# Layer 0 of a four-layer convolution chain: a step's outputs gathered in one block behind the next step's first scores, hidden units on four banks, two key turns together

## The chip, the cores and the metric

The program runs on one core of one Trainium2 chip. The metric is the device time of one execution in microseconds (us); lower is better. The kernel before was timed three times: 6459.06 us is the median, 6456.72 and 6465.38 us are the ends. One more execution was profiled and took 6479.63 us.

## What is computed

Four layers run one after the other on an image batch x of 4 x 16 x 512 x 512 floats. The change touches layer 0 alone:

```python
x = x + depthwise_conv3x3(x)                  # "position"
xt = tokens(x)
q, k, v = qkv(affine1(xt)), in 8 x 8 windows, 2 heads of 8 channels
x = xt + proj(softmax(q k^T / sqrt(8)) v)     # attention within each window
x = x + fc2(gelu(fc1(affine2(x))))            # 16 -> 64 -> 16 channels
```

Layer 1 quantizes its input (by the largest absolute value of layer 0's output), convolves, normalizes by batch statistics and clips; layers 2 and 3 are convolutions with additions. They take the second half of the time and are not changed.

## The kernel before, in words

**Tiling.** `window_attention` (L154) computes layer 0. The image is cut into 64 steps (`STEPS`, L177). A step holds 256 windows: 128 partitions are 4 strips `vv` of 32, and along the free dimension lie 4 images `u` of 512 tokens each (8 windows of 64). PSUM has eight banks: `bank(0)` to `bank(3)` are two pairs, `bank(4)` to `bank(7)` are singles (L182 to L186).

**The parts of a step n**, in the order in which they are written out by hand (loop at L469; the schedule of TensorE, VectorE, ScalarE and SyncE is manual, L451, so each engine works through its instructions in the order of the text):

- `values(k, n)` (L342), for k = 0 to 7: four 128 x 128 transposes of the keys' tile `y2` on TensorE into bank 4 or 6, then a copy on VectorE into `yt`.
- `scores(k, n)` (L355): sixteen matmuls with tiles of 32 rows by 128 columns into banks 0 to 3, then two exponentials of 1024 columns on ScalarE.
- `attend(k, n)` (L374): sixteen matmuls of 128 rows by 32 columns for the weighted sums and four more for the denominators; `divide` (L389): a logarithm and an exponential on ScalarE, one product on VectorE.
- The loop for k = 1 to 7 (L479) writes scores of k, attend of k - 1, values of k, divide of k - 1. So TensorE has scores, attend, values in turn. At odd k `turn_keys` (L316) sends eight DMAs on SyncE's queue, which bring the next step's keys into `y2`.
- `queries` (L326) for the next step, twice, and `project` (L399), both with tiles of 32 x 32.
- The second half, here called the unit stretch (L506 to L515): 52 places. A place is either a `hidden` unit (L412: four matmuls of 32 x 32 tiles into one of the banks 4, 5, 6, then a Gelu on ScalarE) or four matmuls of the depthwise convolution of step n + 2 (L291, banks 0 to 3). Places go round the four row groups of the array. Hidden units stand at places 4, 7, 10 and so on, every third; there are 16 of them and 36 depthwise places.
- `output` (L425): four matmuls of 128 rows by 32 columns into bank 7, then an addition on VectorE into `xo`; in odd steps `store` (L437) follows: one maximum over 1024 columns on VectorE (L439) and sixteen DMAs on SyncE's queue to the DRAM tile `x1` (L96). Outputs stand at four points of a step: after hidden units 5 and 9, behind the unit stretch, and (the last four hidden units) behind the next step's first scores (L476).
- `position(n + 2)` (L302) empties banks 0 to 3: two of them on VectorE, two on ScalarE. ScalarE loads the table for exponentials at L471, after that, and the Gelu table with the first Gelu of a step.

After the last step a bound on the scores is computed (L523 to L535, with two reductions over partitions on GpSimd); a flag from it decides whether another attention routine runs. Then the convolution layers start.

Of the kernel before, what the change touches and what calls it, by code (L numbers as in the profile page):

```python
# [1 line left out]

# [22 lines left out]
P = 128  # L25
# [5 lines left out]
NH, HD = 2, 8  # L31
WS = 8
# [51 lines left out]
        nc.sync.dma_start(part[:, at : at + m, :], src[:, a : a + m, :])  # L84


def _store_block(nc, x1, src, b, r0, cols):

    n = WS // 2
    s, m = divmod(r0 // 2, M)  # L90
    parts = [(1, m, s, 0, n), (0, m + 1, s, 0, n)]
    if m + n == M and s < S - 1:
        parts[1:] = [(0, m + 1, s, 0, n - 1), (0, 0, s + 1, n - 1, 1)]
    for r, mm, ss, at, k in parts:
        part = 32 * b + C * r
        nc.sync.dma_start(  # L96
            x1[mm : mm + k, part : part + C, ss, cols].rearrange("m c x -> c m x"),
            src.rearrange("c (m r) x -> c m r x", r=2)[:, at : at + k, 1 - r],
        )
# [54 lines left out]
def window_attention(ctx: ExitStack, tc, xw, x1, hots, m, v, peak):  # L154
# [78 lines left out]
    with tc.tile_pool(name="w0s", bufs=1) as scratch:  # L233
# [10 lines left out]
        size = wts.tile([P, NH + 1], F32, name="size")  # L244
# [27 lines left out]
    px = ctx.enter_context(tc.tile_pool(name="w0x", bufs=2))  # L272
# [69 lines left out]
    def values(k, n):  # L342

        vv, jl = k // 2, 4 * (k % 2)
        b = bank(4 + 2 * (k % 2))
        for jj in range(4):
            nc.tensor.transpose(  # L347
                b[:, P * jj : P * jj + P],
                y2[:, vv, jl + jj].rearrange("p w t -> p (w t)"), m("ident"),
            )  # L350
        t = px.tile([P, 4, P], F32, tag="yt", name=f"yt{n}_{k}", bufs=3)
        nc.vector.tensor_copy(t.rearrange("p j c -> p (j c)"), b)  # L352
        return t

    def scores(k, n):  # L355

        vv, jl = k // 2, 4 * (k % 2)
        for jj in range(4):
            for u in range(U):
                nc.tensor.matmul(  # L360
                    bank(u)[:, P * jj : P * jj + P],
                    y2[quad(u), vv, jl + jj].rearrange("p w t -> p (w t)"),
                    g[quad(u), vv, jl + jj].rearrange("p h t -> p (h t)"),
                    start=True, stop=True,
                )
        e = px.tile([P, U, 4, P], F32, tag="e", name=f"e{n}_{k}", bufs=3)
        for i in range(2):
            nc.scalar.activation(  # L368
                e[:, 2 * i : 2 * i + 2].rearrange("p u j t -> p u (j t)"),
                pairs[i], AF.Exp,  # L370
            )
        return e

    def attend(e, yt, k):  # L374

        b, d = bank(4 + 2 * (k % 2)), bank(5 + 2 * (k % 2))
        for jj in range(4):
            for u in range(U):
                nc.tensor.matmul(  # L379
                    b[quad(u), P * jj : P * jj + P], yt[:, jj, quad(u)], e[:, u, jj, :],  # L380
                    start=True, stop=True,
                )
        for u in range(U):
            nc.tensor.matmul(  # L384
                d[quad(u)], own, e[:, u].rearrange("p j t -> p (j t)"),
                start=True, stop=True,
            )
# [21 lines left out]
                y[:, u], bank(4 + u), pb, y[:, u], ALU.add, ALU.add  # L409
            )  # L410

    def hidden(y, q, n):  # L412

        u, vv = q // 4, 3 * q % 4
        b = bank(4 + q % 3)
        for k in range(4):
            nc.tensor.matmul(  # L417
                b[quad(k)], fc1[quad(vv), quad(k)], y[quad(vv), u, :],
                start=True, stop=True,
            )  # L420
        hd = px.tile([P, N], F32, tag="hid", name=f"hid{n}_{u}_{vv}", bufs=8)
        nc.scalar.activation(hd, b, AF.Gelu, bias=f1b)  # L422
        return vv, hd

    def output(y, xo, hids, u, n):  # L425
        b = bank(7)
        for vv, hd in hids:
            nc.tensor.matmul(b[quad(vv)], m("fc2"), hd, start=True, stop=True)  # L428
        at = BW * (n % 2)
        nc.vector.tensor_tensor(  # L430
            xo[:, u, :, at : at + BW].rearrange("p a (j x) -> p a j x", x=WS),
            by_window(b), by_window(y[:, u]), ALU.add,
        )
        if n % 2:
            store(xo, n // 2, u)

    def store(xo, k, u):  # L437
        i, cb = divmod(k, NQ)
        nc.vector.tensor_reduce(  # L439
            peak[:, U * k + u : U * k + u + 1], xo[:, u], AX.XY, ALU.max,  # L440
            apply_absolute_value=True,
        )
        for vv in range(V):
            for w in range(2):
                r = SR * (2 * vv + w) + WS * i
                _store_block(
                    nc, x1, xo[32 * vv + C * w : 32 * vv + C * w + C, u], u, r,
                    slice(XW * cb, XW * cb + XW),
                )

    ctx.enter_context(  # L451
        tc.manual_schedule(
# [13 lines left out]
    for h in range(NH):  # L466
        queries(ys[0], h)
    last, xo = None, None
    for n in range(STEPS + 1):  # L469
        if n < STEPS:  # L470
            nc.scalar.preload_act_table_set("natural_log_exp_and_others")  # L471
# [5 lines left out]
        if n == STEPS:  # L477
            break
# [44 lines left out]
    top = wts.tile([P, 1], F32, name="top")  # L523
    nc.vector.tensor_reduce(top, most, AX.X, ALU.max)
    ytop = wts.tile([P, 1], F32, name="ytop")
    nc.gpsimd.partition_all_reduce(ytop, top, P, bass_isa.ReduceOp.max)
    sized = wts.tile([P, NH + 1], F32, name="sized")
    nc.gpsimd.partition_all_reduce(sized, size, P, bass_isa.ReduceOp.add)
    bound = wts.tile([P, 1], F32, name="bound")
    nc.vector.tensor_tensor(bound, sized[:, 0:1], sized[:, 1:2], ALU.max)  # L530
    nc.vector.tensor_scalar(bound, bound, ytop, sized[:, 2:3], ALU.mult, ALU.add)
    nc.vector.tensor_scalar(bound, bound, ytop, 1.0 / 8.0, ALU.mult, ALU.mult)
    flag = wts.tile([P, 1], mybir.dt.int32, name="flag")
    nc.vector.tensor_scalar(flag, bound, 40.0, None, ALU.is_le)
    return nc.values_load(flag[0:1, 0:1], min_val=0, max_val=1)  # L535


# [816 lines left out]
```

## Time and profile before

| What | us |
|---|---|
| median of three runs | 6459.06 |
| the profiled execution | 6479.63 |
| its span | 6477.8 |
| first transposes of layer 0's step 1 and of step 63 start at | 122.6 and 3479.5 |
| one step, from transposes to transposes | 54.12 |
| layer 0's last output matmuls start at | 3539.8 |
| last stores of layer 0 issued until | 3564.3 |
| first VectorE instruction of the convolution layers at | 3568.8 |

TensorE's matmul row is busy for 96% of the span, VectorE for 50%, ScalarE for 63%. A busy matmul row doesn't mean that TensorE does as much as it can: matmuls overlap, and their ends are modelled. The row of weight loads (PEld) tells more, since every matmul has its own load right ahead of it; where loads stop, TensorE can't take the next instruction. A 32-bit matmul appears as two loads and two matmul records. In the timeline each line gives the start, the duration, the engine, the source line, the operation with the shape of its tile (rows by columns of the array), what is written and read, the number of instructions, and in brackets how long the engine was idle before and what ended that.

Between steps 2 and 61 every step has the same pattern, and nearly every one takes 54.10 to 54.15 us. Its parts, read from the starts of the weight loads of one such step:

| Part of a step | us |
|---|---|
| values 0, scores 0, output of the step before, scores 1 | 0.59, 1.38, 1.25, 2.00 |
| attend 0 with denominators | 1.87 |
| six times values, scores, attend | 6 x 3.56 |
| values 7, queries, attend 7, queries and project | 0.59, 1.07, 1.90, 3.90 |
| unit stretch in three pieces | 6.25, 3.40, 5.57 |
| the outputs behind these pieces | 1.00 each |

### The profile page before, as it was taken

What the parts mean: (1) busy time and instruction counts of PE and PEld (TensorE: products, weight loads), DVE (VectorE), ACT (ScalarE), POOL (GpSimd) and SP (SyncE); (2) the same over time, 40 slices, a digit from 0 to 9 for tenths busy, and PEclk for the clock granted to TensorE, in tenths of its full rate; (3) what the DMA queues carried; (4) which work ended last, traced back from release to release, by engine and by line L of the source; (5) the groups of instructions that cost most, each with busy time, mean ns of one, the idle gap of its engine ahead of it and who ended that gap; (6) DMA issues with size and microseconds to landing.
All of it is one profiled execution on the core that took longest, in us unless ns stands there. A gap on an engine that the chain in (4) does not pass through costs nothing. (4 is left out here: it accounts for less than half of the span.)

```text
span 6477.8 us, 317011 instructions
## 1 busy us (share of the span) xinstructions
PE 6215.1 (96%) x146976; PEld 3422.4 (53%) x146976; DVE 3208.4 (50%) x4713; ACT 4062.8 (63%) x5602; POOL 130.9 (2%) x89
## 2 busy tenths in 40 slices
PE   8999999999999999999998569999999999999999
PEld 4555555555555555555553335555555555555554
DVE  3444444444444444444443564555555555555555
ACT  4777777777777777777775443444444444444444
POOL 0000000000000000000000520000000000000000
PEclk9999999999999999999998679999999999999999
DMA  3333333333333333333232752222222222222221
GB/s 80 62 72 61 72 61 72 61 72 61 72 61 72 60 73 61 72 60 73 59 58 36 295 181 75 83 82 82 83 84 86 81 81 81 81 86 82 83 74 51
DMA packets 568966, 515.30 MB, mean 80 GB/s; under 512 B 349008, under 2 KB 480208, under 8 KB 547152
## 3 DMA queue, kind: packets, MB, share of 16 engines
q1 hardware_dynamic: 567344, 494.52, 29.4%
q8 instruction: 1154, 18.91, 1.2%
q14 instruction: 180, 1.47, 0.1%
q10 hardware_dynamic: 288, 0.39, 0.0%
HBM read 225.87 MB, written 134.48 MB: 56 GB/s over the span
## 5 line engine op out<-in xcount | busy, mean ns | idle before, releaser
L1139 PE MATMUL tb<-y,mat 32*32 32x512 f32 x16384 | 1494.9, 596 | 6.5 <-issue 6.0
L1145 ACT ACTIVATE hid<-tb,vec 128x512 f32<-128x512 f32 x1280 | 829.5, 688 | 1068.3 <-PE tb L1139 1066.1
L368 ACT ACTIVATE e<-pair 128x1024 f32<-128x1024 f32 x1024 | 992.3, 1021 | 225.7 <-PE pair L360 225.0
L296 PE MATMUL pair<-x,taps 32*32 32x512 f32 x18432 | 968.2, 606 | 1.8 <-ACT y L307 1.2
L1147 DVE TENSOR_SCALAR hid<-tb,vec 128x512 f32<-128x512 f32 x768 | 574.4, 748 | 745.1 <-PE tb L1139 737.3
L417 PE MATMUL bank<-y,fc_e 32*32 32x512 f32 x8192 | 878.5, 607 | 3.7 <-ACT hid L422 3.1
L422 ACT ACTIVATE hid<-bank,f1b 128x512 f32<-128x512 f32 x1024 | 679.4, 686 | 298.4 <-PE bank L417 284.7
L352 DVE COPY yt<-bank 128x512 f32<-128x512 f32 x512 | 353.7, 691 | 905.6 <-PE bank L347 905.6
L360 PE MATMUL pair<-g,y 32*128 32x128 f32 x16384 | 652.1, 285 | 39.7 <-ACT e L368 38.7
L909 PE MATMUL tb<-z,cw 32*32 32x512 f32 x12864 | 634.6, 599 | 5.3 <-issue 4.1
L360 PEld LDWEIGHTS pair<-g,y 32*128 32x128 f32 x16384 | 541.4, 186 | 186.0 <-ACT e L368 108.8
L296 PEld LDWEIGHTS pair<-x,taps 32*32 32x32 f32 x18432 | 459.2, 103 | 288.5 <-issue 183.6
L1139 PEld LDWEIGHTS tb<-y,mat 32*32 32x32 f32 x16384 | 464.1, 103 | 270.7 <-issue 152.5
L909 PE MATMUL tb<-h,cw 32*32 32x512 f32 x12672 | 571.1, 597 | 3.5 <-ACT z L1078 1.5
L909 PE MATMUL tb<-q,cq 32*32 32x512 bf16 x12672 | 424.2, 458 | 151.3 <-issue 98.9
L909 PE MATMUL tb<-x,cw 32*32 32x512 f32 x12480 | 562.5, 597 | 2.0 <-ACT z L1078 1.4
L379 PE MATMUL bank<-e,yt 128*32 128x128 f32 x16384 | 555.3, 276 | 0.9 <-ACT r L394 0.9
L384 PE MATMUL bank<-e,hot 128*32 128x512 f32 x4096 | 534.4, 592 | 0.0
L379 PEld LDWEIGHTS bank<-e,yt 128*32 128x32 f32 x16384 | 417.7, 109 | 108.1 <-DVE yt L352 52.8
L1155 PE MATMUL tb<-hid,mat 128*32 128x512 f32 x4096 | 452.7, 594 | 0.0
L430 DVE TENSOR_TENSOR xo<-bank,y 128x512 f32<-128x512 f32 x256 | 177.0, 691 | 546.6 <-PE bank L428 544.7
L347 PEld LDWEIGHTS bank<-mat,y 128*128 128x128 f32 x2048 | 215.1, 141 | 430.1 <-issue 376.5
(158 smaller groups left out, 6731.7 us busy)
## 6 DMA issues: line engine op xcount, KB each, us to landing
x<-in_xw_dram SPq DMA_DIRECT2D x32, 2600.0 KB, 10.2
y<-y SPq DMA_DIRECT2D x2048, 32.0 KB, 2.1
tx<-x SPq DMA_DIRECT2D x64, 1024.0 KB, 5.7
xi<-x SPq DMA_DIRECT2D x1024, 64.0 KB, 2.1
out_dram<-xi SPq DMA_DIRECT2D x64, 1024.0 KB, 5.9
x<-xo SPq DMA_DIRECT2D x2000, 32.0 KB, 1.7
y<-x SPq DMA_DIRECT2D x24, 1024.0 KB, 5.5
xi<-x SPq DMA_DIRECT2D x24, 1024.0 KB, 5.2
```

The costliest lines, as they stand in the source:

```text
L296: nc.tensor.matmul(bank(u)[quad(vv)], taps[quad(u), tap, :], xts[n // 2][quad(u), vv, dy : dy + WS, at : at + BW], start=tap == 0, stop=ta ...
L360: nc.tensor.matmul(bank(u)[:, P * jj : P * jj + P], y2[quad(u), vv, jl + jj].rearrange("p w t -> p (w t)"), g[quad(u), vv, jl + jj].rearra ...
L368: nc.scalar.activation(e[:, 2 * i : 2 * i + 2].rearrange("p u j t -> p u (j t)"), pairs[i], AF.Exp,)
L379: nc.tensor.matmul(b[quad(u), P * jj : P * jj + P], yt[:, jj, quad(u)], e[:, u, jj, :], start=True, stop=True,)
L384: nc.tensor.matmul(d[quad(u)], own, e[:, u].rearrange("p j t -> p (j t)"), start=True, stop=True,)
L417: nc.tensor.matmul(b[quad(k)], fc1[quad(vv), quad(k)], y[quad(vv), u, :], start=True, stop=True,)
L422: nc.scalar.activation(hd, b, AF.Gelu, bias=f1b)
L909: nc.tensor.matmul(p[i][_quad(j)], weights[_quad(i), side, dx, :], src[side][_quad(i), j, dx : dx + W], start=side == 0 and dx == 0, stop= ...
L1139: nc.tensor.matmul(p[_quad(c)], w1[_quad(b), 1 - par, 32 * c : 32 * c + 32], inner(ys(mm + par))[_quad(b), s, :], start=True, stop=True,)
L1145: nc.scalar.activation(hd, p, AF.Relu, bias=v("l3_b1"))
L1147: nc.vector.tensor_scalar(hd, p, v("l3_b1"), 0.0, ALU.add, ALU.max)
L1155: nc.tensor.matmul(p[_quad(b), :], w2[:, par], hd, start=par == 0, stop=par == 1)
```

## The change

- A step's sixteen output matmul groups (four per image, all four images) stand in one block, into banks 5, 7, 4 and 6, behind the next step's first scores. Only the last step keeps its outputs between its hidden units, in banks 0 to 3.
- Hidden units go round four banks (4 to 7) rather than three, and stand at places 4, 6, 9, 11, 14, 16, 19, 21 and so on (gaps of 2 and 3 in turn), so that the last of them is at place 41 rather than 49. The tiles of hidden values get 16 buffers rather than 8.
- The transposes of k = 0 and k = 1 stand together at the start of a step; those of k = 1 no longer stand behind attend 0.
- The maximum over `xo` is put off: one of the four goes behind `divide` at k = 1, 2, 4 and 5 of the following step.
- The table for exponentials is loaded behind the last Gelu and ahead of `position`, rather than behind it.
- The bound and the flag are computed ahead of the last step's unit stretch.
- The last 64 stores (76 DMAs) go to the queues of SyncE and GpSimd in turn.

The number of matmuls of every kind stays as it was. In the diff, cut to its core:

```diff
+        (next(queues) if queues else nc.sync).dma_start(
...
-    def hidden(y, q, n):
+    def hidden(y, q, vv, n):
-        u, vv = q // 4, 3 * q % 4
-        b = bank(4 + q % 3)
+        u, b = q // 4, bank(4 + q % 4)
...
-    def output(y, xo, hids, u, n):
-        b = bank(7)
-        for vv, hd in hids:
-            nc.tensor.matmul(b[quad(vv)], m("fc2"), hd, start=True, stop=True)
+    def output(y, xo, hids, us, banks, n):
+        for k, (vv, hd) in enumerate(hids):
+            nc.tensor.matmul(
+                bank(banks[k // 4])[quad(vv)], m("fc2"), hd, start=True, stop=True
+            )
         at = BW * (n % 2)
+        for u, i in zip(us, banks):
+            nc.vector.tensor_tensor(
+                xo[:, u, :, at : at + BW].rearrange("p a (j x) -> p a j x", x=WS),
+                by_window(bank(i)), by_window(y[:, u]), ALU.add,
+            )
+            if n % 2:
+                store(xo, n // 2, u)
+    queues = itertools.cycle((nc.sync, nc.gpsimd))
+    largest = []
...
-    for n in range(STEPS + 1):
-        if n < STEPS:
-            nc.scalar.preload_act_table_set("natural_log_exp_and_others")
-            yts = {0: values(0, n)}
-            es = {0: scores(0, n)}
+    nc.scalar.preload_act_table_set("natural_log_exp_and_others")
+    for n in range(STEPS):
+        yts = {k: values(k, n) for k in range(2)}
+        es = {0: scores(0, n)}
         if last:
             output(*last)
         for k in range(1, 8):
             es[k] = scores(k, n)
             attend(es[k - 1], yts[k - 1], k - 1)
-            yts[k] = values(k, n)
+            if k > 1:
+                yts[k] = values(k, n)
             divide(k - 1, n)
...
+            elif largest:
+                largest.pop(0)()
...
+        if n + 1 == STEPS:
+            flag = bounded()
+        at = [4 + 10 * u + d for u in range(U) for d in (0, 2, 5, 7)]
         hids, taken = [], [0] * U
         for i in range(13 * 4):
-            q, rest = divmod(i - 4, 3)
-            if i >= 4 and rest == 0 and q < 16:
-                hids.append(hidden(y, q, n))
-                if q in (5, 9):
-                    output(y, xo, hids[q - 5 : q - 1], q // 4 - 1, n)
+            if i in at:
+                q = len(hids)
+                hids.append(hidden(y, q, i % 4, n))
+                if n + 1 == STEPS and q in (5, 9, 13):
+                    u = q // 4 - 1
+                    output(y, xo, hids[q - 5 : q - 1], (u,), (u,), n)
             elif ahead:
                 depthwise(n + 2, taken[i % 4], i % 4)
                 taken[i % 4] += 1
+        if n + 1 < STEPS:
+            nc.scalar.preload_act_table_set("natural_log_exp_and_others")
         if ahead:
             ys[n + 2] = position(n + 2)
-        output(y, xo, hids[8:12], 2, n)
-        last = (y, xo, hids[12:], U - 1, n)
+        last = (y, xo, hids, range(U), (5, 7, 4, 6), n)
+    output(y, xo, hids[12:], (3,), (3,), n)
+    for f in largest:
+        f()
```

More of the change, by code (lines that the diff above doesn't have):

```diff
@@ L1 @@
+import itertools
 from contextlib import ExitStack
@@ L84, in _load_rows, with _store_block @@
         nc.sync.dma_start(part[:, at : at + m, :], src[:, a : a + m, :])
-def _store_block(nc, x1, src, b, r0, cols):
+def _store_block(nc, x1, src, b, r0, cols, queues=None):
     n = WS // 2
@@ L95, in _store_block @@
         part = 32 * b + C * r
-        nc.sync.dma_start(
+        (next(queues) if queues else nc.sync).dma_start(
             x1[mm : mm + k, part : part + C, ss, cols].rearrange("m c x -> c m x"),
@@ L420, in hidden @@
             )
-        hd = px.tile([P, N], F32, tag="hid", name=f"hid{n}_{u}_{vv}", bufs=8)
+        hd = px.tile([P, N], F32, tag="hid", name=f"hid{n}_{u}_{vv}", bufs=16)
         nc.scalar.activation(hd, b, AF.Gelu, bias=f1b)
         return vv, hd
-    def output(y, xo, hids, u, n):
-        b = bank(7)
-        for vv, hd in hids:
-            nc.tensor.matmul(b[quad(vv)], m("fc2"), hd, start=True, stop=True)
-        at = BW * (n % 2)
[L430 to L435, printed above, removed]
+    def output(y, xo, hids, us, banks, n):
[3 more added lines that the diff above has]
+            )
+        at = BW * (n % 2)
+        for u, i in zip(us, banks):
[7 more added lines that the diff above has]
+    largest = []
     def store(xo, k, u):
         i, cb = divmod(k, NQ)
-        nc.vector.tensor_reduce(
-            peak[:, U * k + u : U * k + u + 1], xo[:, u], AX.XY, ALU.max,
-            apply_absolute_value=True,
+        largest.append(
+            lambda: nc.vector.tensor_reduce(
+                peak[:, U * k + u : U * k + u + 1], xo[:, u], AX.XY, ALU.max,
+                apply_absolute_value=True,
+            )
         )
@@ L447, in store, with bounded @@
                     nc, x1, xo[32 * vv + C * w : 32 * vv + C * w + C, u], u, r,
-                    slice(XW * cb, XW * cb + XW),
+                    slice(XW * cb, XW * cb + XW), queues if k == STEPS // 2 - 1 else None,
                 )
+    def bounded():
+        top = wts.tile([P, 1], F32, name="top")
+        nc.vector.tensor_reduce(top, most, AX.X, ALU.max)
+        ytop = wts.tile([P, 1], F32, name="ytop")
+        nc.gpsimd.partition_all_reduce(ytop, top, P, bass_isa.ReduceOp.max)
+        sized = wts.tile([P, NH + 1], F32, name="sized")
+        nc.gpsimd.partition_all_reduce(sized, size, P, bass_isa.ReduceOp.add)
+        bound = wts.tile([P, 1], F32, name="bound")
+        nc.vector.tensor_tensor(bound, sized[:, 0:1], sized[:, 1:2], ALU.max)
+        nc.vector.tensor_scalar(bound, bound, ytop, sized[:, 2:3], ALU.mult, ALU.add)
+        nc.vector.tensor_scalar(bound, bound, ytop, 1.0 / 8.0, ALU.mult, ALU.mult)
+        flag = wts.tile([P, 1], mybir.dt.int32, name="flag")
+        nc.vector.tensor_scalar(flag, bound, 40.0, None, ALU.is_le)
+        return flag
     ctx.enter_context(
@@ L468, in window_attention @@
     last, xo = None, None
-    for n in range(STEPS + 1):
-        if n < STEPS:
-            nc.scalar.preload_act_table_set("natural_log_exp_and_others")
-            yts = {0: values(0, n)}
-            es = {0: scores(0, n)}
+    nc.scalar.preload_act_table_set("natural_log_exp_and_others")
+    for n in range(STEPS):
+        yts = {k: values(k, n) for k in range(2)}
+        es = {0: scores(0, n)}
         if last:
             output(*last)
-        if n == STEPS:
-            break
         for k in range(1, 8):
@@ L515, in window_attention @@
                 taken[i % 4] += 1
+        if n + 1 < STEPS:
+            nc.scalar.preload_act_table_set("natural_log_exp_and_others")
         if ahead:
             ys[n + 2] = position(n + 2)
-        output(y, xo, hids[8:12], 2, n)
-        last = (y, xo, hids[12:], U - 1, n)
[L523 to L534, printed above, removed]
+        last = (y, xo, hids, range(U), (5, 7, 4, 6), n)
+    output(y, xo, hids[12:], (3,), (3,), n)
+    for f in largest:
+        f()
     return nc.values_load(flag[0:1, 0:1], min_val=0, max_val=1)
```

## The prediction

> **What bounds the kernel now.** I read the busy shares and the slices first, then the timeline of one step by engine, then the waits.
>
> ```profile
> PE 6215.1 (96%) x146976; PEld 3422.4 (53%) x146976; DVE 3208.4 (50%) x4713; ACT 4062.8 (63%) x5602; POOL 130.9 (2%) x89
> PE   8999999999999999999998569999999999999999
> ```
>
> TensorE is the engine in layer 0 (slices 1 to 22), but 96% doesn't say how much of that is work. The weight loads at a step's end do:
>
> ```profile
> 1030.76 0.16 PEld L428 LDWEIGHTS bank<-hid,mat 128*32 128x32 f32 x8 [0.84 <-issue]
> 1031.75 0.15 PEld L296 LDWEIGHTS pair<-x,taps 32*32 32x32 f32 x12 [0.84 <-issue]
> ...
> 1041.71 0.16 PEld L428 LDWEIGHTS bank<-hid,mat 128*32 128x32 f32 x8 [0.84 <-issue]
> 1042.71 0.42 PEld L347 LDWEIGHTS bank<-mat,y 128*128 128x128 f32 x4 [0.84 <-ACT hid L422]
> 1043.30 1.26 PEld L360 LDWEIGHTS pair<-g,y 32*128 32x128 f32 x32 [0.17 <-issue]
> 1044.68 0.16 PEld L428 LDWEIGHTS bank<-hid,mat 128*32 128x32 f32 x8
> 1045.93 0.30 PEld L360 LDWEIGHTS pair<-g,y 32*128 32x128 f32 x4 [1.09 <-ACT e L368]
> 1046.84 0.97 PEld L360 LDWEIGHTS pair<-g,y 32*128 32x128 f32 x28 [0.61 <-ACT e L368]
> 1047.93 0.81 PEld L379 LDWEIGHTS bank<-e,yt 128*32 128x32 f32 x32
> 1048.72 0.24 PEld L384 LDWEIGHTS bank<-e,hot 128*32 128x32 f32 x8
> 1049.80 0.42 PEld L347 LDWEIGHTS bank<-mat,y 128*128 128x128 f32 x4 [0.84 <-issue]
> 1050.39 0.98 PEld L360 LDWEIGHTS pair<-g,y 32*128 32x128 f32 x32 [0.17 <-issue]
> ```
>
> Two things are to be seen. Where the tile's shape changes, loads stop (0.84 us). And the second scores (1045.93 and 1046.84) wait for the exponentials of the first, which come late because of what ScalarE has ahead of them:
>
> ```profile
> 1041.69 0.69 ACT L422 ACTIVATE hid<-bank,f1b 128x512 f32<-128x512 f32 x1 [0.28 <-PE bank L417]
> 1042.28 1.26 ACT L307 ACTIVATE y<-pair,vec 128x512 f32<-128x512 f32 x2
> 1043.56 1.28 ACT L471 ACT_TABLE_LOAD   x1
> 1044.85 1.94 ACT L368 ACTIVATE e<-pair 128x1024 f32<-128x1024 f32 x2
> ```
>
> A block of the new size isn't in layer 0, but the last layer has one of 32 matmuls, with the same tile shape:
>
> ```profile
> 5027.17 0.16 PEld L1155 LDWEIGHTS tb<-hid,mat 128*32 128x32 f32 x8 [0.84 <-DVE x L1106]
> 5027.63 0.13 PEld L1155 LDWEIGHTS tb<-hid,mat 128*32 128x32 f32 x4 [0.30 <-issue]
> ...
> 5033.20 0.13 PEld L1155 LDWEIGHTS tb<-hid,mat 128*32 128x32 f32 x4 [0.30 <-issue]
> 5034.17 0.27 PEld L909 LDWEIGHTS tb<-z,cw 32*32 32x32 f32 x32 [0.84 <-DVE xi L1159]
> ```
>
> From 5027.17 to 5034.17 it takes 7.00 us for 16 rounds of four: 0.43 us a round (two rounds for four 32-bit matmuls) and 0.13 us once, for the change of shape.
>
> **What the Trainium skill says.** "TensorEngine Tiling (Array Packing)", Key Properties: changing the tiling mode, not just the tile, drains TensorE. The trace agrees: no load crosses a change of shape, and each costs 0.13 to 0.15 us beyond the matmuls. "TensorE: Matmul & The Clock Gate", Architectural detail: the queue is 64 deep and can pull weight loads ahead of running matmuls; here sixteen tiles with two loads and two matmuls each just fill it. "ScalarE: Activation LUTs", What ACT_TABLE_LOAD costs: about 1283 ns for the load; the trace has 1283 ns for all.
>
> **The change part by part**, for a steady step (54.12 us).
>
> (1) *One block of outputs.* Before: three blocks of 1.00 us (1030.76 to 1031.75) and one of 1.25 (1044.68 to 1045.93, 0.25 of it waiting): 4.25. After: eight rounds of 0.43 and 0.13: 3.57. **-0.68.** Its additions (0.69 us each on VectorE) keep up with 0.86 us per image; banks 4 and 6 must first be copied to `yt`, which VectorE has done by about 2.6 us after the step's start, while the block reaches bank 4 at about 4.2.
>
> (2) *The second scores no longer wait.* The first exponentials end about 2.1 us after the first scores; the block of 3.57 us covers that. Scores took 2.00 us where they waited and take 1.10 elsewhere (1050.39 to 1051.49). **-0.90.** If the cover were gone, this comes back.
>
> (3) *The unit stretch in one piece.* Its pieces of 12 and 20 places took 3.40 and 5.57 us: 8 more places cost 2.17, so a round of four costs 1.085 and an end 0.145. Two ends go: 15.22 becomes 14.93. **-0.29.** A fourth bank gives nothing by itself: the waits of hidden units for Gelus are 6.5 us in 59 steps, and at the start of the program depthwise places alone (207 loads in 6.86 us) run at 1.06 a round. TensorE sets this pace, not the banks.
>
> (4) *Closer turns and the earlier table.* The last hidden unit moves from place 49 to 41. With 0.271 us a place, a start of about 0.65 (the wait for project and y) and 1.1 from a unit's start to its Gelu (seen at places not delayed), it starts its Gelu at about 12.9; 16 Gelus back to back from 2.7 on (0.63 us each: six in 3.82 us) would reach 12.2 to 12.8. So the table is loaded by about 15.0, just when TensorE ends the stretch. `position` on ScalarE (1.26 us) then ends 1.3 us after the stretch; transposes take 1.01 now, and the first scores wait some 0.35 us for it, against 0.28 before. **+0.07.** This is what ScalarE can spoil.
>
> (5) *Two key turns together.* Four transposes and the change cost 0.59, of which 0.42 are loads. Joining saves 0.17. **-0.17.** But the third scores lose a cover: they come 2.97 us after the second ones (1.10, 0.79, 1.08), where the steady spacing is 3.56, and the second exponential of 1024 columns ends at 1.20 + 1.94 = 3.14 after them, plus a semaphore. **+0.23.** Together about nothing.
>
> (6) *Maxima put off.* VectorE has 2.1 us idle in each 3.56 us of the attention part; 1.22 us fits. Cost nothing while k has only a copy and a product (1.4 us).
>
> (7) *Stores as one run.* SyncE's queue issues 64 stores in 36.31 us and the key turns at 0.70 each:
>
> ```profile
> 1032.63 36.31 SPq L96 DMA_DIRECT2D x<-xo  x64
> 1069.05 13.37 SPq L319 DMA_DIRECT2D y<-y  x19
> ```
>
> They used to start 10 us ahead of the even step; now about 4.4 us into it. They end at 40.7; the first eight key turns are issued by 46.2 and landed (2.5 us) by 48.7; the next step needs them at 52.4. The other turns have over 6 us. So **0**, with 3.7 us in hand. The load of the next input slides from 50 to 63 us, and its data are needed a step and a half later. `xo` is written again at 56, its stores have landed by 43.
>
> Sum: -0.68 - 0.90 - 0.29 + 0.07 - 0.17 + 0.23 = **-1.74 us a step**, to 52.38; for 61 steps 106 us, and 0.5 in step 0.
>
> (8) *Last two steps.* Step 62 has no depthwise places. From its first hidden load to the second scores of step 63 it takes 22.2 us; after, ScalarE's 16 Gelus, transposes, scores and the block make about 16.2. TensorE may run at a slower clock there (its blocks of 1.00 us took 1.86), so I take -5. Step 63: hidden units in four banks rather than three, four at a time between outputs: last addition about 4.4 us earlier.
>
> (9) *Last stores on two queues.* SyncE's queue was the limit: 76 DMAs from 3525.67 for 38.63 us, 21 us past the last addition. No DMA of GpSimd's queue is in the trace. Bounds: if GpSimd issues as fast as SyncE, 19 us go; the price in "DMA: Bandwidth & Descriptors", Latency and other measured facts (first byte about 1 us from GpSimd against 0.6) makes an estimate of 37 to 38 us for its half, and nearly nothing goes. I take -10, both ends kept. The flag computed earlier was hidden behind the stores anyway: 0.
>
> Total: 106 + 0.5 + 5 + 4.4 + 10 = 126 us. The profiled execution took 6479.6 us, 0.3% over the median; it becomes 6354, and the median **6333**.
>
> **The rivals.**
>
> *ScalarE takes over the unit stretch (15%).* Hidden units come at 2.5 places, 0.68 us, and a Gelu takes 0.63 to 0.69. If Gelus lag by one more microsecond, the table, `position` and the first scores move by 0.9, and the gain is 0.85 a step: 52 us and the 20 once, 6387. For it: TensorE and ScalarE are within 0.1 us. Against: the ten depthwise places behind the last unit (2.7 us).
>
> *More than reckoned (18%).* Rounds go at 1.06, the third scores find their banks free, GpSimd issues well: 2.3 a step and 27 once: 6291. For it: the bare depthwise rounds.
>
> *The key turns come late (4%), slower.* If stores in one run issue at 0.75 us rather than 0.567 (single ones show over 1.3), they end at 52.4, the first keys land at 60.4, 8.0 late every second step; less the 3.5 gained in two steps this costs 4.5, 31 times, less the 20 gained once: about +120, 6580. It decides from about 0.69 us a store on; below 0.62 it costs nothing. Against: 0.567 was measured in an unbroken run of the same 64.
>
> **How the numbers follow.** Forecast 60%, rivals 15, 18 and 4, unexplained 3. The forecast's own range is 6310 to 6365 (0.3 us a step, the bounds of 9). To hold eight in ten: 6288 to 6380. Within 0.2% (13 us, about what a measurement of this kernel can tell from no change) falls only a mixture of late keys and gains: 2%. Faster 94%, slower 4%.
>
> **What would show it.** Right: steps of about 52.4 us; one L428 block of 3.57 with additions at 0.86; scores behind it at 1.10; a piece of 52 places in 14.9; third scores waiting 0.2 for the exponential. Wrong: transposes at a step's start waiting for a DMA (late keys), first scores waiting over 0.5 us for ScalarE, a GpSimd queue that ends long after SyncE's.

## The result

| | before | after |
|---|---|---|
| median of 4 runs each, side by side, us | 6462.22 | 6375.64 |
| ratio, with its 95% interval | | 0.9867 (0.9848 to 0.9886) |
| one profiled execution: span, us | 6477.8 | 6371.6 |
| median step of layer 0 (steps 1 to 57), us | 54.12 | 52.68 |
| time over the median step, summed over steps 1 to 57, us | 0.7 | 7.3 |
| steps 58 to 62, us | 54.11 54.12 54.12 54.13 55.07 | 54.44 53.31 56.59 54.65 53.69 |
| first VectorE instruction of the convolution layers at, us | 3568.8 | 3475.0 |
| from there to the end, us | 2909.0 | 2896.6 |

The changed kernel is faster by 87 us. 126 us were forecast, and a time of 6333, so 6375.64 lies only 4 us inside the upper end of the range (6380). It is nearer to 6387, the number of the rival in which ScalarE takes over the unit stretch, than to the forecast's own. Layer 0 became 94 us shorter in the profiled executions. The last row is not the change's doing: that code is the same, and over all the profiled runs of this study it took between 2886 and 2909 us. I therefore read layer 0 by the start of the convolution layers and by the median step.

The profile's summary still shows TensorE busy for 96% of the span, though the span is 106 us shorter. The share says nothing here; the weight loads do.

```profile
PE 6125.4 (96%) x146976; PEld 3619.7 (57%) x146976; DVE 3189.7 (50%) x4713; ACT 4035.4 (63%) x5602; POOL 151.0 (2%) x127
```

The timeline of TensorE's weight loads at the start of step 18 of the changed kernel (L348 are transposes, L361 scores, L428 outputs, L380 the weighted sums):

```profile
1016.80 0.86 PEld L348 LDWEIGHTS bank<-mat,y 128*128 128x128 f32 x8 [0.84 <-issue]
1018.13 0.30 PEld L361 LDWEIGHTS pair<-g,y 32*128 32x128 f32 x4 [0.47 <-ACT y L308]
1018.78 0.97 PEld L361 LDWEIGHTS pair<-g,y 32*128 32x128 f32 x28 [0.36 <-ACT y L308]
1019.88 0.16 PEld L428 LDWEIGHTS bank<-hid,mat 128*32 128x32 f32 x8
...
1022.48 0.13 PEld L428 LDWEIGHTS bank<-hid,mat 128*32 128x32 f32 x4 [0.30 <-issue]
1023.45 0.98 PEld L361 LDWEIGHTS pair<-g,y 32*128 32x128 f32 x32 [0.84 <-issue]
1024.55 0.81 PEld L380 LDWEIGHTS bank<-e,yt 128*32 128x32 f32 x32
1026.42 1.29 PEld L361 LDWEIGHTS pair<-g,y 32*128 32x128 f32 x32 [0.84 <-ACT e L369]
```

The block of outputs stands from 1019.88 to 1023.45, 3.57 us, and the scores behind it take 1.10 us (to 1024.55) without a wait. Both are as forecast. The two waits of the first scores for `y L308`, ScalarE's half of `position`, are not: 0.47 and 0.36 us, 0.83 together, where the prediction had named over 0.5 us as a sign of being wrong. ScalarE and VectorE just before that:

```profile
1015.18 1.28 ACT L549 ACT_TABLE_LOAD   x1
1016.60 1.41 DVE L312 TENSOR_SCALAR y<-pair,vec 128x512 f32<-128x512 f32 x2 [11.02 <-PE pair L297]
1017.39 1.34 ACT L308 ACTIVATE y<-pair,vec 128x512 f32<-128x512 f32 x2 [0.92 <-DVE y L312]
1019.80 1.94 ACT L369 ACTIVATE e<-pair 128x1024 f32<-128x1024 f32 x2 [1.07 <-PE pair L361]
```

ScalarE has its table by 1016.46. Its first copy then starts only at 1017.39, and what releases it, by the profile, is VectorE's first copy. Each engine reads a bank of its own, but the two banks belong to one pair tile. I took it that the program makes the second reader of the tile wait for the first; the first experiment tests it.

Part by part, medians over steps 5 to 56:

| Part of a step | before | forecast | after |
|---|---|---|---|
| transposes and scores ahead of the outputs, with those of k = 1 (us) | 2.56 | 2.46 | 3.08 |
| outputs | 4.25 | 3.57 | 3.57 |
| second scores | 2.01 | 1.10 | 1.10 |
| third scores | 1.10 | 1.33 | 1.41 |
| unit stretch without outputs | 15.22 | 14.93 | 14.51 |
| step | 54.12 | 52.38 | 52.68 |

Some of the parts went better than forecast and some worse, and the step is only 0.30 us off because these misses partly cancel. Two more differences are not in the median step. First, the last row of blocks is stored in 76 pieces a step rather than 64, which pushes back the key turns behind them in SyncE's queue. That queue in step 62, and what TensorE waits for in the last 375 us of layer 0 (total, times, longest):

```profile
3354.01 41.80 SPq L97 DMA_DIRECT2D x<-xo  x76
3395.92 16.25 SPq L320 DMA_DIRECT2D y<-y  x23
```

```profile
PE bank L348 <- DMA y<-y: 10.2, 3, 4.7
```

The key turns of step 62 begin 47 us after its start, and TensorE waits for the keys at the end of steps 58, 60 and 62.

Second, TensorE runs out of instructions now and then in odd steps. In step 17 the input load (2.6 MB) is issued at 977.51, and the sums over weights stop at 985.8 with nothing in the program to wait for:

```profile
985.01 0.81 PEld L380 LDWEIGHTS bank<-e,yt 128*32 128x32 f32 x30
986.51 0.11 PEld L380 LDWEIGHTS bank<-e,yt 128*32 128x32 f32 x1 [0.69 <-issue]
```

The DMA records show instructions arriving in packets of 16 KB, one each 4 to 8 us; between 974.4 and 984.3 none starts, while the load has the DMA engines (share 0.88 to 0.98 from 978 to 984). There are 1154 such packets for TensorE's 295007 instructions, about 256 in each. Between 200 and 3150 us TensorE's matmuls stop for over 0.2 us without a wait in the program five times. All five stops come a whole multiple of 256 instructions apart, and TensorE goes on 1.3 to 1.6 us after a packet has landed. So it stops where a packet ends, for want of the next one.

The tail of layer 0, the last stores on two queues:

```profile
3448.16 22.27 SPq L97 DMA_DIRECT2D x<-xo  x38
3448.45 13.14 POOL L97 DMA_DIRECT2D x<-xo  x25 [3.43 <-DVE xo L433]
3461.76 6.64 POOL L97 DMA_DIRECT2D x<-xo  x13 [0.17 <-issue]
```

GpSimd takes 0.52 us a DMA on average, SyncE 0.59.

### The profile page after: what moved, and what is told of

It reads as the page before. It is cut to its first block, busy times and chain, and to the rows that moved or that the text cites. A ratio compares the mean times of both kernels' runs of the same rounds, so it can differ in the third digit from the quotient of the medians.

```text
span 6371.6 us, 316872 instructions
## 1 busy us (share of the span) xinstructions
PE 6125.4 (96%) x146976; PEld 3619.7 (57%) x146976; DVE 3189.7 (50%) x4713; ACT 4035.4 (63%) x5602; POOL 151.0 (2%) x127
## 3 DMA queue, kind: packets, MB, share of 16 engines
q8 instruction: 1154, 18.91, 1.3%
## 5 line engine op out<-in xcount | busy, mean ns | idle before, releaser
L297 PE MATMUL pair<-x,taps 32*32 32x512 f32 x18432 | 927.9, 605 | 2.4 <-ACT y L308 1.2
L417 PE MATMUL bank<-y,fc_e 32*32 32x512 f32 x8192 | 680.3, 598 | 1.3 <-DVE y L409 0.9
L361 PE MATMUL pair<-g,y 32*128 32x128 f32 x16384 | 654.0, 285 | 27.1 <-ACT y L308 24.5
L361 PEld LDWEIGHTS pair<-g,y 32*128 32x128 f32 x16384 | 544.1, 187 | 216.1 <-issue 110.8
L297 PEld LDWEIGHTS pair<-x,taps 32*32 32x32 f32 x18432 | 601.8, 103 | 98.5 <-issue 18.8
L422 ACT ACTIVATE hid<-bank,f1b 128x512 f32<-128x512 f32 x1024 | 644.2, 686 | 13.0 <-PE bank L417 5.5
L380 PE MATMUL bank<-e,yt 128*32 128x128 f32 x16384 | 557.4, 276 | 3.6 <-issue 2.1
L396 DVE TENSOR_TENSOR o<-bank,r 128x512 f32<-128x512 f32 x512 | 354.3, 692 | 372.4 <-ACT r L395 356.2
L380 PEld LDWEIGHTS bank<-e,yt 128*32 128x32 f32 x16384 | 418.2, 109 | 112.4 <-DVE yt L353 52.8
L312 DVE TENSOR_SCALAR y<-pair,vec 128x512 f32<-128x512 f32 x128 | 90.3, 747 | 707.1 <-PE pair L297 707.1
```

The source lines that it names most:

```text
L297: nc.tensor.matmul(bank(u)[quad(vv)], taps[quad(u), tap, :], xts[n // 2][quad(u), vv, dy : dy + WS, at : at + BW], start=tap == 0, stop=ta ...
L361: nc.tensor.matmul(bank(u)[:, P * jj : P * jj + P], y2[quad(u), vv, jl + jj].rearrange("p w t -> p (w t)"), g[quad(u), vv, jl + jj].rearra ...
L380: nc.tensor.matmul(b[quad(u), P * jj : P * jj + P], yt[:, jj, quad(u)], e[:, u, jj, :], start=True, stop=True,)
L417: nc.tensor.matmul(b[quad(k)], fc1[quad(vv), quad(k)], y[quad(vv), u, :], start=True, stop=True,)
```

## The experiments

All are edits of the changed kernel. They ran in three groups, and each ratio is to the kernel before, run beside it; the changed kernel's own ratio is 0.9867. "Start" is that of the convolution layers in the profiled execution (changed kernel: 3475.0).

| Run | median us | ratio (interval) | median step | over it, steps 1 to 57 | start |
|---|---|---|---|---|---|
| position by pairs | 6337.80 | 0.9798 (0.9781 to 0.9814) | 52.12 | 5.9 | 3442.1 |
| key turns apart | 6390.08 | 0.9877 (0.9861 to 0.9894) | 52.96 | 7.8 | 3491.0 |
| last row of blocks on two queues | 6356.86 | 0.9834 (0.9817 to 0.9850) | 52.68 | 5.0 | 3461.6 |
| load on ScalarE's queue | 6461.22 | 1.0000 (0.9991 to 1.0009) | | | 3558.9 |
| three banks | 6405.57 | 0.9899 (0.9883 to 0.9916) | 53.14 | 5.9 | 3505.4 |
| old places | 6448.87 | 0.9963 (0.9949 to 0.9977) | 53.47 | 16.8 | 3535.8 |
| table late | 6379.51 | 0.9854 (0.9838 to 0.9871) | 52.68 | 5.6 | 3476.8 |
| query copies by pairs | 6347.73 | 0.9804 (0.9787 to 0.9820) | 52.22 | 7.3 | 3450.2 |
| last stores on one queue | 6391.62 | 0.9888 (0.9872 to 0.9903) | 52.68 | 6.2 | 3494.7 |
| load in odd steps | 6416.55 | 0.9924 (0.9910 to 0.9937) | 53.27 | 22.6 | 3529.1 |
| four edits joined | 6341.61 | 0.9810 (0.9797 to 0.9824) | 52.47 | 12.6 | 3447.2 |
| and all stores on two queues | 6342.22 | 0.9811 (0.9798 to 0.9825) | 52.35 | 24.2 | 3445.7 |

The intervals of key turns apart, three banks, last row of blocks on two queues, table late and last stores on one queue overlap with that of the changed kernel. What these five show is read from their traces, not from the whole time. In the last three rows odd and even steps differ, and the median lies between two groups: it stands for no step.

### Position by pairs

```diff
         for u in range(U):
-            if u % 2:
+            if u >= 2:
                 nc.scalar.activation(
```

> Position empties the first pair of banks on VectorE and the second on ScalarE, instead of one bank of each pair on each. Theory: in the changed kernel ScalarE, idle for 0.92 us after the table load, waits for VectorE because both read the same pair; that puts 0.62 us per step into the first transposes and scores (1.33 and 1.75 us where 1.01 and 1.45 were forecast). Without it the two together fall from 3.08 to about 2.3 us, a step from 52.67 to about 51.9, the whole by about 45 us to some 6330. Rival, ScalarE's Gelus and table are what is late: ScalarE starts position no earlier, the change stays under 5 us.

The step went from 52.68 to 52.12 us. The timeline of weight loads at the start of such a step:

```profile
1006.86 0.86 PEld L348 LDWEIGHTS bank<-mat,y 128*128 128x128 f32 x8 [0.84 <-issue]
1008.13 1.13 PEld L361 LDWEIGHTS pair<-g,y 32*128 32x128 f32 x32 [0.41 <-DVE y L312]
1009.38 0.16 PEld L428 LDWEIGHTS bank<-hid,mat 128*32 128x32 f32 x8
```

From transposes to outputs it takes 2.52 us instead of 3.08, against the 2.46 of my forecast. ScalarE no longer waits for VectorE:

```profile
1006.97 1.26 ACT L308 ACTIVATE y<-pair,vec 128x512 f32<-128x512 f32 x2 [0.45 <-PE pair L297]
```

It still waits 0.45 us for TensorE's last matmuls of the stretch, so about half of the 0.92 us was the order. The same four copies are made, two on each engine; only which engine takes which bank differs. So the lost 0.6 us was the order between two readers of one tile. The step falls short of the 51.9 that I expected, since the first scores now wait 0.41 us for VectorE's copies.

### Query copies by pairs

```diff
         for vv in range(V):
             out = g[:, vv, :, h, :]
             src = bank(vv).rearrange("p (j t) -> p j t", t=T)
-            if vv % 2:
+            if vv >= 2:
```

> Queries' results leave the first pair of banks on VectorE and the second on ScalarE, as e1 did for position. Theory: ScalarE's wait of 1.42 us for VectorE in each of two query rounds is the same sharing of a pair; the last logarithm and exponential of a step then come about 0.6 us earlier, and project's second half and the second queries with them: -0.5 to -0.8 us a step, -30 to -50 us. Rival, these waits are beside TensorE's path: under 5 us.

The same wait stands in `queries`, where it was before the change too (in the changed kernel, "ACT g L338" waits 1.4 us for "DVE g L340" at each of 112 places between 200 and 3150 us of the span). The second half of the queries and the project now take 3.48 us rather than 3.91, and the step 52.22. This shows that the loss belongs to this way of sharing a tile, and not to `position` in particular.

### Key turns apart

```diff
-        yts = {k: values(k, n) for k in range(2)}
+        yts = {0: values(0, n)}
...
-            if k > 1:
-                yts[k] = values(k, n)
+            yts[k] = values(k, n)
```

> The transposes of k = 1 go back behind attend 0. Theory: the eight transposes are hidden in the wait for position, so taking four away there saves nothing; 0.59 us comes back in the loop and the third scores lose their 0.31 us wait: +0.28 us a step, +17 us. Rival (the forecast's own ledger): joined and apart are worth the same, apart even 0.06 us better per step, 0 to -4 us.

The step is 0.28 us longer. Four transposes at the start take the same 1.33 us as eight, because the scores behind them wait for `position` anyway. So joining the turns saves the whole piece of 0.59 us, and costs the third scores 0.31 (1.41 to 1.10).

### Three banks, and the old places

```diff
-        u, b = q // 4, bank(4 + q % 4)
+        u, b = q // 4, bank(4 + q % 3)
```

> Hidden units go round three banks (4, 5, 6) at the new, closer places. Theory: at gaps of 2 and 3 places a hidden unit comes every 0.67 us, and three banks allow one in about (1.1 + 0.69 + 0.07) / 3 = 0.62 us only while nothing is queued behind Gelus; counted place by place the unit stretch grows by 0.8 to 0.9 us and the last Gelu comes 0.4 us later: +50 to +60 us. Rival (a sentence of the forecast: the fourth bank gives nothing by itself): 0 to +5 us.

```diff
-        at = [4 + 10 * u + d for u in range(U) for d in (0, 2, 5, 7)]
+        at = [4 + 3 * q for q in range(16)]
```

> Hidden units at the old places, every third one up to 49, with four banks and everything else as changed. Theory: the last Gelu then ends at about 15.4 us of the unit stretch and the table is loaded at 16.7, against 14.5 where TensorE ends; position on ScalarE starts 1.3 to 1.6 us later than in the changed kernel and the first scores with it: a step of about 54.1, +80 to +100 us. Rival, ScalarE has that much to spare or TensorE's stretch gets shorter by it: under +20 us.

With three banks the stretch takes 14.93 us; the fourth bank is what shortens it to 14.51. The step grows by 0.46, less than I expected, but not by the rival's nothing. The weight loads of the hidden units, first with three banks, then in the changed kernel (busy and mean, then the idle time before them and what ended it, 200 to 3150 us of the span):

```profile
L417 PEld LDWEIGHTS bank<-y,fc_e 32*32 32x32 f32 x7152 | 196.6, 103 | 86.9 <-DVE y L409 13.7 <-ACT hid L422 9.0
L417 PEld LDWEIGHTS bank<-y,fc_e 32*32 32x32 f32 x7168 | 233.1, 103 | 54.2 <-DVE y L409 13.7
```

The waits named sum to much less than the idle time, because this view names only those over 0.15 us. With the shorter ones counted, the loads wait for a Gelu at eight places of a step, 0.82 us in all; with four banks at one place, 0.09 us. That covers the 0.42. With the old places (below), as before the change, there is no such wait: it is the closer places that make the fourth bank worth having. That 14.93 is also the figure of my forecast is chance, since the forecast had no waits for banks in it.

With the old places and four banks the stretch is no longer than with the new ones (14.38). The loss comes after it: transposes and first scores take 3.99 us rather than 3.08. ScalarE's last Gelus come later, so the table and `position` do, and the first scores wait for them; the waits of TensorE between 200 and 3150 us:

```profile
PE pair L361 <- ACT y L308: 67.8, 55, 1.3
```

The closer places are thus worth 0.79 us a step, 49 us in 62 steps; with the time over the median step, of which this run had 10 us more, the convolution layers start 61 us later, less than the 80 to 100 I expected.

### Table late

```diff
-        if n + 1 < STEPS:
-            nc.scalar.preload_act_table_set("natural_log_exp_and_others")
         if ahead:
             ys[n + 2] = position(n + 2)
+        if n + 1 < STEPS:
+            nc.scalar.preload_act_table_set("natural_log_exp_and_others")
```

> The table for exponentials is loaded behind position again, as before the change. Theory: position can't use the earlier moment, since ScalarE waits for VectorE there, and the block of outputs covers exponentials that come 0.2 us later: 0, within 4 us. Rival (the change's order is needed): the second scores wait for the exponentials, 0.3 to 1.3 us a step, +20 to +80 us.

Nothing changes: 52.68 us. Its 1.28 us lie in ScalarE's time either way, before its wait for VectorE or behind `position` while TensorE works on the scores.

### Last row of blocks on two queues

```diff
-                    ... queues if k == STEPS // 2 - 1 else None,
+                    ... queues if k >= STEPS // 2 - NQ else None,
```

> The stores of the last four pairs of steps, not only of the last, go to the queues of SyncE and GpSimd in turn. Theory: in steps 58, 60 and 62 the 76 store DMAs (64 elsewhere) push the key turns past the start of the next step, TensorE waits 1.7, 3.9 and 4.7 us and then runs at half clock for a while; with half of the stores elsewhere the waits go, layer 0 is 10 to 13 us shorter. Rival, the waits have another cause (SyncE's queue is delayed by something else, or GpSimd's stores block): the three waits stay or grow.

Steps 58 to 62 become 52.67, 52.68, 52.68, 52.67 and 49.86 us, and the convolution layers start 13.5 us earlier. So the stores of those rows made the keys late, and behind them the gain forecast for step 62 appears: 5.2 us less than before.

### Last stores on one queue

```diff
-                    ... queues if k == STEPS // 2 - 1 else None,
+                    ... None,
```

> The changed kernel, with the last 64 stores (76 DMAs) on SyncE's queue alone. Theory (the second queue halves the time to issue them, as the trace of the changed kernel shows with 22.3 us and 19.8 us side by side): 76 DMAs at 0.55 us take 42 us from the same start, so the convolution layers start about 20 us later than in the changed kernel (near 3495), and the whole is about 20 us slower. Rival (the gain of the last 30 us came from outputs that are ready earlier, and one queue would have followed them): less than 8 us slower.

```profile
3450.68 39.30 SPq L97 DMA_DIRECT2D x<-xo  x76
```

The layers start at 3494.7, 19.7 us later. From step 63's start to that point it takes 89.1 us, as in the kernel before (89.4), against 72.2 with two queues. So the earlier outputs of the last step bring nothing by themselves: the queue was the limit, and all 17 us of the last step come from the second one.

### Load on ScalarE's queue

```diff
-        nc.sync.dma_start(t, xw[k])
+        (nc.scalar if k > 1 else nc.sync).dma_start(t, xw[k])
```

> The input load is issued from ScalarE's queue ahead of the Gelus instead of from SyncE's behind stores and key turns. Theory: the odd steps' stalls of 0.2 to 1.4 us (8 us in all) are TensorE out of instructions, because the load of 2.6 MB, now issued 14 us into an odd step, holds back the fetch of instructions there; with the load some 40 us into the even step those stalls go from that place: -5 to -8 us, if the fetch is not hit elsewhere. Rival: a load of 10 us hits the fetch wherever it stands, or delays the key turns: stalls move, or the next step's first transposes wait for a DMA; 0 to +50 us.

I had expected ScalarE to have room for it. Instead the convolution layers start 84 us later than in the changed kernel, more than the rival's 50 as well, and two causes are mixed. The issue of the load waited on ScalarE for the stores of `xo` (about 3 us ahead of the Gelu table), so the Gelus came late: weight loads of hidden units waited 56.5 us for them between 200 and 3150 us of the span, up to 3.6 at once. And the load met the unit stretch, where TensorE ran out of instructions: its weight loads of the depthwise convolution lost 73 us there without a wait in the program (12 in the changed kernel), up to 2.6 at once. Odd steps, now without a load, fell from 52.94 to 52.59 us on average, as expected; even steps took 53.8 to 58.6 us and the whole gain was gone.

### Load in odd steps

```diff
-        if ahead and n % 2 == 0 and n // 2 + 2 < STEPS // 2:
-            xts[n // 2 + 2] = load(n // 2 + 2)
+        if ahead and n % 2 and (n + 3) // 2 < STEPS // 2:
+            xts[(n + 3) // 2] = load((n + 3) // 2)
```

> The changed kernel, with the load of the next input (2.6 MB) issued in the second half of every odd step, behind that step's key turns, rather than in the second half of the even step, where the stores and key turns queued ahead of it hold it until the attention part of the odd step. Theory (in the changed kernel TensorE stands still for 0.2 to 1.4 us in odd steps because its instructions are fetched late while the load has the DMA engines): the load falls into the unit stretch as in the kernel before, which lost 0.7 us in all to such stops; the 7 to 8 us over the median step in steps 1 to 57 go down to under 2, the median step stays at 52.67, the whole is 5 to 8 us faster. Rival (the stops come with any load, and the unit stretch is only luckier, or they are not the load's): the sum stays at 5 or more, the whole within 3 us.

My expectation was wrong: the layers start 54 us later than in the changed kernel, not a little earlier. Odd steps now take 53.7 to 57.3 us, all of them, and even ones 52.4 to 52.9. In a step whose load is issued at 1014.01, at the head of the unit stretch, the weight loads stop for over 3 us, and the windows (us, then busy time and count of each engine, granted TensorE clock, DMA share, GB/s) show what else goes on:

```profile
1020.06 0.15 PEld L417 LDWEIGHTS bank<-y,fc_e 32*32 32x32 f32 x4
1023.32 0.11 PEld L417 LDWEIGHTS bank<-y,fc_e 32*32 32x32 f32 x2 [3.12 <-issue]
```

```profile
1014.00:1020.00 6.00, 6.00 (x200) 4.43 (x192) 2.94 (x5) 5.12 (x8) 0.00 (x0) 1.00 0.88 324
1020.00:1023.30 3.30, 1.11 (x32) 0.21 (x9) 0.00 (x0) 1.59 (x3) 0.00 (x0) 1.00 0.56 232
1023.30:1026.00 2.70, 2.68 (x62) 1.23 (x65) 0.00 (x0) 1.08 (x2) 0.00 (x0) 0.58 0.02 6
```

While the load moves, no packet of instructions starts between 1012.0 and 1021.1. After the stop TensorE works at 0.58 of its clock for a while.

The Trainium skill, "TensorE: Matmul & The Clock Gate", section Why this matters for your kernels, warns of gaps over about 3 us between bursts of matmuls, after which the clock falls to half. Here less was enough: the weight loads stopped for 3.1 us, but the matmuls, by their records, for 2.2, and the granted clock was 0.50 for 3.4 us from 1023.7. The same followed a stop of 1.8 us in this run, and none of the shorter ones between 200 and 3150 us.

So the theory that the load is what starves TensorE stands. The stops moved with it: there are 27 of them between 200 and 3150 us, as many as loads, all at the end of a packet (to within one instruction), and TensorE goes on 1.2 to 1.5 us after one has landed. That the unit stretch is the safe place for it is false. Why the kernel before lost only 0.7 us is open. Its load (50 us into an even step) met the last 4 us of the stretch, and the longest gap between packets in the 12 us behind the issue of a load was 6.7 to 9.2 us there, not much shorter than in the changed kernel (7.3 to 10.9), but none of its matmuls stopped.

### The edits joined

> The changed kernel with four edits together: position and the copies of the queries share their banks by pair (one engine has both banks of a pair), the stores of the last row of blocks go on two queues, and the input load is issued in odd steps. Theory (each removes a loss of its own): -0.55 a step from position, -0.45 from queries, so 51.67 us a step, 12 us from the late keys of the last steps, 5 from the load: about 6295 us, 80 us below the changed kernel. Rival (ScalarE, with its first copies earlier or later, becomes the limit in one of the two places, so they don't add up): the step stays above 51.95, and the whole above 6310.

> As the run with four edits together, but every step's stores go on the queues of SyncE and GpSimd in turn, not those of the last row of blocks alone. Theory (in ordinary steps the keys come in time anyway, with 2 us or more in hand): the same time within 3 us. Rival (some of the short stops left in even steps are late keys or stores in the way of the turns): 5 to 10 us faster. Second rival (GpSimd's issuing of 32 DMAs beside VectorE's work in the attention part slows VectorE, and outputs or copies come late): slower by 10 us or more.

The first is `position` and queries by pairs, the last row of blocks on two queues, and the load in odd steps; in the second all stores go on two queues. Steps that issue no load take 51.73 us (even ones, and 61), as the theory has it: 52.68 less 0.56 and 0.46 is 51.66. Those with the load take 53.55 on average, so the misplaced load costs about 1.8 us every second step, 53 us in 29 of them, and hides the rest. The second run is equal to the first: beyond the last rows, the store queue isn't a limit.

The fastest kernel that ran is the one with `position` by pairs alone, 6337.8 us, 2.0% below before and 0.7% below the changed kernel; query copies by pairs and the joined edits are within its interval. The three good edits with the load left where the change put it weren't run. From the joined run, less 53 us and plus the 7 lost around the load in the changed kernel, I estimate some 6295 us.

## Why the forecast was right in kind and its gain 40 us too large

**(1) and (2) hold to the hundredth**: one block of 3.57 us, and second scores of 1.10. The durations came from the same shapes elsewhere in the trace before.

**(3) was mis-sized**, by 0.42 us to the good. "A fourth bank gives nothing by itself" is false at the new places: three banks give 14.93 us there, four 14.51. I took the waits for Gelus from the old places, where units come every third place and the loads wait for none; at gaps of two and three places they do. The price of a round (1.085) was too high as well: with the old places and four banks, where the loads wait for no Gelu either, the stretch takes 14.38. The bare depthwise rounds (1.06) named in the rival were the better measure. What made rounds quicker there, the fourth bank or the stretch in one piece, was not run apart.

**(4) is the step that failed most.** I let `position` on ScalarE begin at the end of the stretch, and reckoned +0.07. ScalarE was ready, but waited 0.92 us until VectorE's first copy was done, and the first scores came 0.6 us late; the pair edit gives 0.56 of it back. Before the change ScalarE came to `position` at 1042.4 in the step shown, behind its last Gelu, when VectorE's first copy (0.7 us from 1041.41) was just done, so that the same order cost nothing and left no wait:

```profile
1041.41 1.41 DVE L311 TENSOR_SCALAR y<-pair,vec 128x512 f32<-128x512 f32 x2 [3.16 <-ACT hid L422]
```

The rival "ScalarE takes over the unit stretch" had the right place and nearly the right number, but the wrong cause: the Gelus ended on time, and the table edit changes nothing.

**(5)** was right that the two effects nearly cancel; each was larger (-0.59 and +0.31). With (4) as it is, the joint start is worth 0.28.

**(6)** cost nothing visible: the maxima fit between VectorE's copies and products.

**(7)** holds for the ordinary even steps, whose eighth key turn was issued by 45.4 to 50.1 us (46.2 forecast), but I reckoned with 64 stores in every step. The blocks of the last row are cut finer, 76 stores (as (9) counts them for the last step), and the 3.7 us in hand were gone: 13 us in five steps. The rival for late keys had the mechanism and tied it to the price of a store; it was the number of stores. The input load, noted as sliding to 63 us with its data due late, was priced at nothing by its due time. What it cost, 7 us, was the time for which it keeps TensorE's instructions waiting.

**(8)** The 5 us of step 62 are there once its keys are on time, and were covered by the late keys. The 4.4 of step 63 and the 10 of **(9)** were added as if independent; together they are 17, and belong to the second queue alone. For (9) the first-byte price of a GpSimd DMA was the wrong quantity: what counts in a run of DMAs is the time between issues, 0.52 us against SyncE's 0.59.

Luck had a part in it: what (3) gave beyond the forecast (0.42) covers more than half of what the first scores (0.62) and the third ones (0.08) lost against it. The sum: 126 forecast, less 17 (0.30 us in 57 steps), 7 (instruction stops), 13 (steps 58 to 62), plus 3 in step 0 (3.2 gained rather than 0.5) and 3 in step 63, makes 95; layer 0 of the profiled executions gained 94. The medians differ by 87, with an interval of 74 to 98.

## What to carry to other kernels

When two engines empty a group of banks, give each engine whole tiles: readers of different banks of one tile were put in an order here, and in `position` that only showed once the second engine came early. Count DMAs for the edge blocks too when a queue has little in hand, and ask of a moved bulk load whether it holds up the arrival of instructions, not only when its data are due. Waits for a resource hold for the schedule in which they were counted, and a view that names only the longer ones can hide a row of short ones: sum the idle time too, and price one more of the resource by a short run.

## What the runs showed of the hardware beyond expectation

- While a load of 2.6 MB moved, up to 10.9 us passed from one packet of TensorE's instructions to the next (usual: 4 to 8), and TensorE stood still for 0.3 to 2.2 us at the end of a packet (its weight loads for up to 3.1); on SyncE's queue this cost between 7 and some 50 us in all, by the place of the load.
- GpSimd issued plain DMAs (26 of 32 KB, 12 smaller) at 0.52 us each in a run; SyncE took 0.52 alone (76 in 39.30 us) and 0.59 beside it.
- After a stop of 2.2 us of its matmuls (3.1 of its weight loads) TensorE ran at 0.58 of its clock in the next 2.7 us; after one of 1.8 us the clock fell as well.
- A fourth PSUM bank in turn made the stretch of the same matmuls 3% shorter (14.93 to 14.51 us): with three, the weight loads of hidden units waited for a Gelu at eight places of a step, seven of them for under 0.15 us.
